# A gated bidirectional scan with a binarised linear layer: adding x to finished batches in six transfers of 512 tokens where there were twelve of 256

## The chip, the core and the metric

The kernel runs on one core of one Trainium2 chip. The time is the device time of one launch in microseconds (us), lower is better; a median of a few runs is given with the lowest and the highest. One more execution was taken with the hardware profiler, and every duration below is from that one. PE is the matrix engine, DVE the vector engine, ACT the scalar (activation) engine, POOL the GpSimd engine, SP the engine that only issues DMAs here. DMAs that SP issues go by one queue, which the profile calls q1 (hardware_dynamic), those that POOL issues by another, q0 (software_dynamic); both are worked off by the same 16 DMA engines.

## What is computed

All arrays are float32; x and the side input are 4 x 1024 x 1024 (batch, token, channel).

```python
def wkv(r, k, v, w, u, time_emb):            # r = x, k = v = side input
    tf = sigmoid(sum(time_emb))              # one number per batch
    decay = exp(-exp(w)) * (0.5 + 0.5 * tf)  # per batch and channel
    ek = exp(min(k, 30)); ekv = ek * v
    nf, df = scan over tokens: a = a * decay + ekv, b = b * decay + ek
    nb, db = the same, from the last token to the first
    euk = exp(min(u + k, 30))
    num = nf + nb - ekv + euk * v
    den = df + db - ek + euk
    return sigmoid(r) * num / max(den, 1e-8) * (0.8 + 0.2 * tf)

bw = where(weight >= 0, 1, -1) * mean(abs(weight), over inputs)
out = x + wkv(x, side, side, w, u, cond) @ bw.T + bias
```

## The kernel before, in words

**Blocks.** The main loop `for g in range(steps)` has 32 steps; block g is one batch (g // 8) and 128 channels (g % 8), with the channels on the partitions and the 1024 tokens along the row. Each block loads a column block of the side input (`load_k`, L102) and of x (`load_gate`, L107) on SP, turns them on PE (L266, L272), takes exponentials on ACT (L278, L284) and runs four scans of 1024 tokens on DVE: numerator forward and backward (L366, L379), denominator forward and backward. Each backward scan starts from one column that ACT computes (`act_edge`, L372, "edge_num" and "edge_den").

**The block before, in the same step.** In step g DVE also finishes the denominator of block g - 1 (L389) and applies its gate (L423). POOL adds the own term of block g - 1 to its numerator by an accumulating DMA (`dma_own_numerator`, L384, 512 KB), floors the denominator (`floor_den`, L396), clamps block g (`pool_clamp`, L346), splits block g - 2 for the matrix product (L438) and multiplies block g - 1 (`den_product` L416, `num_product` L419, `gated_product` L428). ACT takes the reciprocal by a logarithm and an exponential (`act_log` L404, `act_reciprocal` L411) and makes the upper part of block g - 2 (`act_hi`, L433).

**The linear layer.** When the eight blocks of a batch are done, PE forms 16 groups for it, each 512 tokens by 128 outputs (`pe_product`, L449), some two and a half in a step. ACT scales a group and adds the bias (`act_scale`, L461), PE turns it back (`pe_turn`, L469), and ACT copies it into one half of a staged tile (`act_leave`, L557, 512 tokens by 256 outputs). When the second half is in, SP stores the tile to `out` (`store`, L135, 512 KB). The pool `resid` of staged tiles has two buffers, so the first copy into a tile waits until the store before last has landed. The first three batches go this way; what is stored lacks x. The last batch is done after the loop in another form (`pe_wide_product`, L517), and its x is added on DVE.

**Adding x.** For the first three batches POOL issues DMAs that read rows of x and accumulate them into the same rows of `out`, in HBM (`add_x`, L140). The dictionary `adds` says in which step each is issued, two steps or more after the batch's groups: four for each batch, 256 tokens and 1 MB each, in steps 16, 18, 20 and 22 for the first batch and 24, 26, 28 and 30 for the second. The four of the third batch would fall in steps 32 and later and are issued after the loop. In a step, `add_x` stands right behind `dma_own_numerator(g - 1)` in POOL's order.

**Order.** Nothing is reordered: the program runs under `tc.manual_schedule()`, and each engine and each DMA queue takes its instructions in the order of the text. One place depends on `adds`: in a step that issues an add, `act_log` stands behind `act_edge` for the numerator on ACT, in a step without one ahead of it:

```python
if g > 0 and not adds[g]:
    act_log(g - 1)
...
act_edge(g, nums[g], "edge_num")
if g > 0 and adds[g]:
    act_log(g - 1)
```

Of the kernel before, what the change touches and what calls it, by code (L numbers as in the profile page):

```python
# [21 lines left out]
def kernel(  # L22
# [28 lines left out]
    P = 128  # L51
    B, T, C = x.shape
    TD = time_emb.shape[1]
    NT = T // P
    NC = C // P
    H = 512
    NH = T // H
# [4 lines left out]
    rows = ctx.enter_context(tc.tile_pool(name="rows", bufs=2))  # L62
# [73 lines left out]

    def add_x(b, n):

        rows = slice(2 * n * P, 2 * (n + 1) * P)
        nc.gpsimd.dma_start(  # L140
            out=out[b, rows, :], in_=x[b, rows, :], accum_op=ALU.add, max_dma_last_dim=8192
        )
# [418 lines left out]
    steps = B * NC  # L561
# [38 lines left out]

    adds = {g: [] for g in range(steps + 1)}
    for b in range(B - 1):
        for n in range(NT // 2):
            adds[min((b + 2) * NC + 2 * n, steps)].append((b, n))

# [9 lines left out]
    with tc.manual_schedule():  # L617
# [57 lines left out]
        for g in range(steps):  # L675
            b, cc = divmod(g, NC)
# [16 lines left out]
            for i in adds[g]:  # L693
                add_x(*i)
# [100 lines left out]
        for i in adds[steps]:  # L795
            add_x(*i)
# [43 lines left out]
        n = NT - 1  # L840
# [41 lines left out]
```

## Time and profile before

| | |
|---|---|
| time before | 489.85 us, median of 3 runs (489.81 to 491.19) |
| profiled execution: its own time, its span | 489.83 us, 488.0 us |
| busy, share of the span | DVE 97%, POOL 82%, PE 75%, ACT 69% |
| chain that ended last | DVE 75%, PE 17%, issue 3%, ACT 2% |
| x into `out` by accumulating DMA | 12 issues on POOL, 1024 KB each, 11.8 us from issue to landing (median) |
| own terms by accumulating DMA | 32 issues on POOL, 512 KB each, 5.6 us |
| staged tiles to `out` | 24 issues on SP, 512 KB each, 5.1 us |
| bytes moved | q1 59.78 MB, q0 29.37 MB |

The span is the time from the first to the last instruction of the profiled execution; the 1.8 us between it and the execution's time lie outside. A busy share is an average over all stages. The chain that ended last is followed back from the last instruction to whatever released each one, so an engine's share in it says how much of the time it held up the end. In rows of the profile, `out<-in` names what is written and read, and a wait is put down to the last of the things waited for.

### The profile page before, as it was taken

To read this page: it belongs to the slowest core of one execution; us is meant where nothing else is said; L and a number is where in the kernel's file an instruction comes from. 1 tells how busy PE (TensorE), PEld (TensorE's weight loads), DVE (VectorE), ACT (ScalarE), POOL (GpSimd) and SP (SyncE) were. 2 spreads that over 40 slices of the span, in tenths; PEclk is the share of its full clock that TensorE was granted. 3 is DMA by queue.
4 is the path that set the end of the run, shared out by engine and by line. 5 is a ranking of instruction groups with operands and counts; after the bars stand their busy time and mean duration, and the time that the engine had idled before them with its cause. 6 is when DMAs were issued, how large, how long until landed. Compare 5 with 4: busy or idle time off the path is not lost.

```text
span 488.0 us, 5214 instructions
## 1 busy us (share of the span) xinstructions
PE 363.9 (75%) x1813; PEld 296.9 (61%) x1813; DVE 474.9 (97%) x331; ACT 335.9 (69%) x466; POOL 402.2 (82%) x276
## 2 busy tenths in 40 slices
PE   3434433344588877778999998965999998989996
PEld 2333332233466666656777777744888777868885
DVE  6999999999999999999999999999999999999976
ACT  4795968869595967769697879697866979724000
POOL 3379999999999999999999999999999999991000
PEclk9975566666699999999999999985999999999999
DMA  8865565555455555559787996889569697899954
GB/s 227 246 173 146 156 174 141 137 141 140 112 147 150 147 141 139 147 139 254 177 208 161 264 235 173 167 213 221 126 108 277 151 271 213 188 229 284 235 198 176
DMA packets 89762, 89.49 MB, mean 183 GB/s; under 512 B 2660, under 2 KB 80776, under 8 KB 88200
## 3 DMA queue, kind: packets, MB, share of 16 engines
q1 hardware_dynamic: 83320, 59.78, 41.0%
q0 software_dynamic: 6400, 29.37, 31.6%
q8 instruction: 14, 0.23, 0.2%
q14 instruction: 12, 0.10, 0.1%
q10 hardware_dynamic: 16, 0.00, 0.0%
HBM read 55.59 MB, written 29.36 MB: 174 GB/s over the span
## 4 chain that ended last, share of the span: by engine, by line
DVE 75%; PE 17%; issue 3%; ACT 2%; POOL 0%; DMA 0%; SPq 0%; DVEq 0%; POOLq 0%; ACTq 0%
DVE num L379 13%; DVE den L379 13%; DVE den L366 13%; DVE num L366 12%; PE wide L517 8%; DVE den L389 7%; DVE num L350 6%; DVE den L423 6%; PE po L449 5%; DVE euk L356 4%; PE last L517 2%; PE bank L517 1%; PE sgT L272 1%; PE turned L469 1%; PE kT L266 1%
## 5 line engine op out<-in xcount | busy, mean ns | idle before, releaser
L449 PE MATMUL po<-gated,wT 128*128 128x512 f32 x768 | 199.7, 408 | 0.3 <-ACT staged L557 0.3
L449 PEld LDWEIGHTS po<-gated,wT 128*128 128x128 f32 x768 | 141.9, 192 | 30.4 <-ACT staged L557 0.8
L266 PE MATMUL kT<-ident,k_rows 128*128 128x128 f32 x248 | 42.1, 325 | 61.6 <-issue 43.0
L272 PE MATMUL sgT<-ident,sg_rows 128*128 128x128 f32 x256 | 43.2, 324 | 46.4 <-DVE den L423 41.2
L438 POOL TENSOR_TENSOR gated<-num,gated 128x512 fp32r<-128x512 f32 x60 | 75.6, 1280 | 2.4
L266 PEld LDWEIGHTS kT<-ident,k_rows 128*128 128x128 f32 x248 | 33.8, 167 | 69.4 <-issue 51.6
L379 DVE TENSOR_TENSOR_SCAN den<-bank,edge_den,den 128x1024 f32<-128x1024 f32 x32 | 74.8, 2339 | 0.4 <-ACT edge_den L372 0.4
L416 POOL TENSOR_TENSOR den<-den,eu 128x1024 f32<-128x1024 f32 x31 | 73.8, 2380 | 1.4 <-ACT eu L411 1.4
L379 DVE TENSOR_TENSOR_SCAN num<-bank,edge_num,num 128x1024 f32<-128x1024 f32 x32 | 74.8, 2337 | 0.0
L419 POOL TENSOR_TENSOR num<-num,eu 128x1024 f32<-128x1024 f32 x31 | 73.7, 2377 | 0.8 <-DMA num<-euk 0.8
L428 POOL TENSOR_TENSOR num<-den,num 128x1024 f32<-128x1024 f32 x30 | 71.8, 2393 | 2.8 <-DVE den L423 0.5
L366 DVE TENSOR_TENSOR_SCAN den<-bank,den 128x1024 f32<-128x1024 f32 x32 | 72.2, 2258 | 0.0
L366 DVE TENSOR_TENSOR_SCAN num<-bank,num 128x1024 f32<-128x1024 f32 x31 | 70.6, 2277 | 0.0
L272 PEld LDWEIGHTS sgT<-ident,sg_rows 128*128 128x128 f32 x256 | 35.1, 167 | 57.1 <-DVE den L423 29.7
L433 ACT CAST gated<-num 128x512 fp32r<-128x512 f32 x64 | 36.5, 618 | 30.2 <-POOL num L428 25.8
L396 POOL TENSOR_SCALAR den<-den,floor 128x1024 f32<-128x1024 f32 x31 | 36.8, 1188 | 20.7 <-DVE den L389 17.5
L404 ACT ACTIVATE eu<-den,gain 128x1024 f32<-128x1024 f32 (+1 forms) x33 | 36.9, 1121 | 20.8 <-POOL den L396 20.4
L517 PE MATMUL wide<-wT,gated 128*128 128x512 f32 x192 | 45.4, 393 | 2.1 <-POOL gated L438 2.1
L557 ACT COPY staged<-turned 128x512 f32<-128x512 f32 x48 | 27.5, 574 | 21.3 <-PE turned L469 21.3
L517 PEld LDWEIGHTS wide<-wT,gated 128*128 128x128 f32 x192 | 35.8, 188 | 10.2 <-POOL gated L438 2.5
L389 DVE SCALAR_TENSOR_TENSOR den<-eu,top,den 128x1024 f32<-128x1024 f32 (+1 forms) x33 | 41.5, 1260 | 0.0
L356 DVE SCALAR_TENSOR_TENSOR euk<-eu,top,kT 128x1024 f32<-128x1024 f32 x31 | 38.7, 1250 | 0.0
(91 smaller groups left out, 578.9 us busy)
## 6 DMA issues: line engine op xcount, KB each, us to landing
sg_rows<-in_x_dram SPq DMA_DIRECT2D x32, 512.0 KB, 5.9
num<-euk POOLq DMA_DIRECT2D x32, 512.0 KB, 5.6
k_rows<-in_fside_BxSxS_dram SPq DMA_DIRECT2D x31, 512.0 KB, 5.2
out_dram<-staged SPq DMA_DIRECT2D x24, 512.0 KB, 5.1
out_dram<-in_x_dram POOLq DMA_DIRECT2D x12, 1024.0 KB, 11.8
w_rows<-in_L_ffn_weight_dram SPq DMA_DIRECT2D x8, 512.0 KB, 5.7
x_rows<-in_x_dram SPq DMA_DIRECT2D x8, 512.0 KB, 11.5
out_dram<-x_rows SPq DMA_DIRECT2D x7, 512.0 KB, 2.6
```

Source lines behind the costliest of these rows:

```text
L266: nc.tensor.transpose(kT[:, s * P : (s + 1) * P], k_rows[g][:, s, :], ident)
L272: nc.tensor.transpose(t[:, s * P : (s + 1) * P], sg_rows[g][:, s, :], ident)
L356: nc.vector.scalar_tensor_tensor(euk, eus[g], top[:, b, cc : cc + 1], k_ps[g], ALU.min, ALU.mult)
L366: nc.vector.tensor_tensor_scan(t, decay_row(g), t, 0.0, ALU.mult, ALU.add)
L379: nc.vector.tensor_tensor_scan(back, decay_row(g), back, inits[g, which], ALU.mult, ALU.add)
L389: nc.vector.scalar_tensor_tensor(dens[g][:, ts], eus[g][:, ts], top[:, b, cc : cc + 1], dens[g][:, ts], ALU.min, ALU.add,)
L416: engine.tensor_mul(dens[g][:, ts], dens[g][:, ts], eus[g][:, ts])
L419: engine.tensor_mul(nums[g][:, ts], nums[g][:, ts], eus[g][:, ts])
L428: engine.tensor_mul(nums[g][:, ts], dens[g][:, ts], nums[g][:, ts])
L438: engine.tensor_sub(t[:, 1, :], nums[g][:, h * H : (h + 1) * H], t[:, 0, :].bitcast(F32))
L449: nc.tensor.matmul(prods[q], wT[:, cc, oc * P : (oc + 1) * P], gated[b, cc, h][:, i, :], start=(cc == 0 and i == 0), stop=(cc == NC - 1 an ...
L517: nc.tensor.matmul(t, gated[last, cc, h][:, i, s * P : (s + 1) * P], wT[:, cc, cols], start=(cc == 0 and i == 0), stop=(cc == NC - 1 and i ...
```

## The change

Twelve adds of 256 tokens become six of 512 tokens (2 MB each). They are issued in steps 16 and 20 for the first batch, 24 and 28 for the second, and two after the loop for the third. The same rows get the same x. In steps 18, 22, 26 and 30 no add is issued any more, and by the condition quoted above `act_log` stands ahead of `act_edge` there. The order of every other instruction on every engine is as before. POOL's instruction for an add names 256 rows of 2048 elements where it named 128.

```diff
     def add_x(b, n):
 
-        rows = slice(2 * n * P, 2 * (n + 1) * P)
+        rows = slice(n * H, (n + 1) * H)
         nc.gpsimd.dma_start(
             out=out[b, rows, :], in_=x[b, rows, :], accum_op=ALU.add, max_dma_last_dim=8192
         )
...
     adds = {g: [] for g in range(steps + 1)}
     for b in range(B - 1):
-        for n in range(NT // 2):
-            adds[min((b + 2) * NC + 2 * n, steps)].append((b, n))
+        for n in range(NH):
+            adds[min((b + 2) * NC + 4 * n, steps)].append((b, n))
```

Here P = 128, H = 512, NT = 8, NH = 2, NC = 8, B = 4, steps = 32.

## The prediction, made before the changed kernel ran

> **What bounds the kernel now.** I read the page first: busy shares, the chain that ended last, the DMA issues.
>
> ```profile
> span 488.0 us, 5214 instructions
> PE 363.9 (75%) x1813; PEld 296.9 (61%) x1813; DVE 474.9 (97%) x331; ACT 335.9 (69%) x466; POOL 402.2 (82%) x276
> ...
> DVE 75%; PE 17%; issue 3%; ACT 2%; POOL 0%; DMA 0%; SPq 0%; DVEq 0%; POOLq 0%; ACTq 0%
> ...
> out_dram<-staged SPq DMA_DIRECT2D x24, 512.0 KB, 5.1
> out_dram<-in_x_dram POOLq DMA_DIRECT2D x12, 1024.0 KB, 11.8
> ```
>
> DVE works without a break; no DMA is on the chain. So an add costs nothing by its bytes, only by what it makes late for DVE. How much slack there is stands in the timeline; first DVE and POOL in steps 15 (no add) and 16 (add), two views:
>
> ```profile
> 208.76 1.27 DVE L389 SCALAR_TENSOR_TENSOR den<-eu,top,den 128x1024 f32<-128x1024 f32 x1
> 217.77 1.19 DVE L423 SCALAR_TENSOR_TENSOR den<-den,sgT 128x1024 f32<-128x1024 f32 x1
> 222.25 1.28 DVE L389 SCALAR_TENSOR_TENSOR den<-eu,top,den 128x1024 f32<-128x1024 f32 x1
> 231.26 1.19 DVE L423 SCALAR_TENSOR_TENSOR den<-den,sgT 128x1024 f32<-128x1024 f32 x1
> 235.75 1.32 DVE L389 SCALAR_TENSOR_TENSOR den<-eu,top,den 128x1024 f32<-128x1024 f32 x1
> ```
>
> ```profile
> 215.01 2.40 POOL L416 TENSOR_TENSOR den<-den,eu 128x1024 f32<-128x1024 f32 x1
> 222.16 0.89 POOL L384 DMA_DIRECT2D num<-euk  x1
> 222.76 1.19 POOL L140 DMA_DIRECT2D out_dram<-in_x_dram  x1
> 228.80 2.40 POOL L416 TENSOR_TENSOR den<-den,eu 128x1024 f32<-128x1024 f32 x1
> ```
>
> A step lasts from one L389 to the next, 13.50 us. L423 needs L416. Without an add L416 ends at 217.41, 0.36 us before L423; with one at 231.20, 0.06 before it. POOL is nearly a second bound in steps with an add.
>
> Then the DMA queues around the add of step 28 (issued at 385.33, landed 397.3), in the stretch 390 to 395, and ACT and DVE behind it:
>
> ```profile
> q0 software_dynamic: 102, 0.84, 96.9%
> q1 hardware_dynamic: 102, 0.10, 7.7%
> ```
>
> ```profile
> 398.51 0.59 ACT L557 COPY staged<-turned 128x512 f32<-128x512 f32 x1 [3.18 <-PE turned L469]
> 399.00 0.78 ACT L461 ACTIVATE z<-po,wub,out_scale 128x512 f32<-128x512 f32 x1
> ...
> 402.06 0.28 ACT L372 ACTIVATE edge_num<-num,edge 128x1 f32<-128x1 f32 x1
> ```
>
> ```profile
> 402.97 2.34 DVE L379 TENSOR_TENSOR_SCAN num<-bank,edge_num,num 128x1024 f32<-128x1024 f32 x1
> ```
>
> While the add runs, the engines take one packet of q1 (1 KB, of a staged tile's store) for each packet of the add (8 KB): 102 against 102. So the store issued at 386.40 landed 11.75 us later, at 398.15, where the median store takes 5.1. The copy L557 at 398.51 refills that store's buffer (two buffers, so it waits for the store before last). The profile puts its wait on PE, which was ready last, but the store landed only 0.36 us earlier.
>
> **POOL's part.** The issue of a 2 MB add names 256 rows for 128. Issued behind L384, which ends at 223.05, the old one ends at 223.95: 0.90 us for 128 rows. The cheapest issue on POOL, L622 with 8 rows, took 0.58. Twice the rows therefore cost between 0 more (all fixed) and 0.90 (all by rows); I take 0.31, the difference of the two rows, as that is what 120 rows cost. L416 has 0.06, 0.06, 0.23 and 0.04 to spare in steps 16, 20, 24 and 28, so L423 waits 0.25 + 0.25 + 0.08 + 0.27 = 0.85 us in all; by the bounds 0 and 3.2.
>
> Four steps lose their add. Steps 18, 19, 22, 23, 26, 27 and 30 exceed 13.50 by 0.05, 0.09, 0.03, 0.08, 0.05, 0.10 and 0.01 (a late L423 in the add's step, then an L389 of 1.32 to 1.38 us instead of 1.27), and L389 of step 31 by 0.11: 0.5 us comes back. Net of POOL +0.3, bounds -0.5 and +2.7.
>
> ACT's new order in these four (logarithm ahead of the edge) is that of every step without an add: in step 17 the logarithm ended at 239.57, the edge column at 239.75, and the scan that needs it began at 240.37. Nothing, with 0.6 us of cover; beyond that DVE would wait.
>
> **The transfer's part.** Each add gets 128 packets of 8 KB more. Alone, q0 moved 1.28 MB in the stretch 226 to 232, so 1.05 MB takes 4.9 us; beside a store, 102 packets in 5 us, so 6.3 us. What queues behind it:
>
> On q0, the own-term DMA of the next step. After step 16: the add landed at 233.93, would at 238.8, and 0.52 MB more at the same rate end near 241.3; the DMA landed at 241.7 anyway, and POOL's L419 wants it at 244.42. After step 28: 397.3 + 6.3 + 2.5 = 406.1, wanted at 407.00. No wait, with 0.9 us of cover at the tightest.
>
> On q1, loads and stores. Loads are asked for a step and more ahead; the closest, the k load issued at 386.89 (landed 399.98), would land near 407 where PE wants it at 403.1, but the wait on ACT below is as long and covers it. Stores: after step 16 the store of 232.17 has until the copy at 251.01; after step 20 that of 286.35 (landed 289.95) until 299.34, and 289.95 + 6.3 + 2.5 = 298.8 just makes it; around step 24 there are no stores between 327 and 360. After step 28 the store of 386.40 has 0.36 us and gets at least 4.9 more: it lands at 403.05 to 404.4 if it follows the add, and 2.5 us later, up to 406.9, if the own-term DMA, which POOL issues at 398.53 into the same queue as the add, also goes ahead. I take 405.0, the middle. ACT stands in L557 until then, with L461, L433, L404 and L372 queued behind it; L372 ended at 402.34 for a scan at 402.97, so DVE's wait is the landing less 398.51 less 0.63: 3.9 to 7.8 us, at 405.0 it is 5.9. POOL and PE are late by as much and no more.
>
> [...]
>
> The two adds after the loop carry the bytes of the four; those landed by 467.1, 21 us before the end, so nothing.
>
> Sum, on the profiled execution's 489.83 us (span 488.0 and 1.8 outside; the median is 489.85): + 5.9 + 0.3 = 496.0. With the ends of both terms, 3.4 and 10.5, it is 493.2 to 500.3.
>
> **Rivals.** *The store is not held (ends level).* Place: the store of step 28. If q1's packets get more turns beside the longer add than one in two, it lands in time. It decides at 399.1 (398.51 + 0.63): landing before that, DVE waits for nothing and only POOL's +0.3 is left, 490.1 us, at its bounds 489.3 and 492.5. For it: in the stretch 402 to 405 q1 got 583 packets beside 117 of q0, though those were 512-byte loads against 4 KB packets. Against: 102 to 102 with this very kind of store.
>
> *POOL as the bound.* If generating descriptors goes by rows, 0.90 an issue, the four steps cost 2.7 net, beside the 5.9: 498.4 us. For it: four adds issued in a row after the loop ended 0.83 to 0.90 apart, as work by rows would. Against: 0.58 for 8 rows.
>
> *More than one store late.* The store of 286.35 has 0.5 us to spare. If it comes 2 us late, some 1.4 us more, 497.4.
>
> A gain of 1.5 us is not in sight: all steps together exceed 13.50 by 0.8 us.
>
> **How the numbers follow.** A measurement here can tell 0.3%, 1.5 us. One held store: 0.62, time 496.0. Held store and a dear issue or a second late store: 0.13, 497 to 500. Store not held: 0.22, 489.3 to 492.5, mostly within 1.5 us of before. Something that I don't see, to the good: 0.03. So slower 0.77 (with a tenth of the third case, its upper end), same 0.20, faster 0.03. The range 489.7 to 499.0 leaves out the lower third of the third case and the top of the second, some 0.15; the likeliest case's own is 493.2 to 499.
>
> **What would show it.** In the changed profile: ACT's idle time before one L557 in step 29 of 7 us or more, put down to the store's DMA, with a landing of 17 us or more for the store issued at the start of step 28; right behind it DVE idle at L379 for edge_num by 4 to 8 us, the only long idle of DVE in the loop; L423 waiting 0.1 to 0.3 us in steps 16, 20, 24 and 28; adds that land some 17 us after issue; steps 18, 22, 26 and 30 at 13.50. I am wrong if that store lands within 13 us, or if DVE's idle time lies elsewhere, at L423 above all.

## The result, and the profile after

| | before | after |
|---|---|---|
| median | 489.98 us, 4 runs (489.81 to 491.19) | 497.59 us, 4 runs (495.72 to 497.85) |
| profiled execution: its own time, its span | 489.83 us, 488.0 us | 497.68 us, 495.9 us |
| end of the loop (begin of the L389 behind step 31) | 438.00 us | 444.30 us |
| from there to the span's end | 50.0 us | 51.6 us |

The changed kernel is 1.4% slower: ratio 1.0142, interval 1.0112 to 1.0171. Of the profiled 7.9 us, 6.3 are in the loop and 1.6 behind it. The page first: its span, busy shares, chain, the group of the backward numerator scan, and DMA issues.

```profile
span 495.9 us, 5207 instructions
PE 369.0 (74%) x1813; PEld 300.0 (60%) x1813; DVE 475.1 (96%) x331; ACT 335.5 (68%) x466; POOL 396.9 (80%) x270
...
DVE 63%; PE 18%; ACT 7%; DMA 5%; issue 4%; POOL 1%; SPq 0%; POOLq 0%; DVEq 0%; ACTq 0%
...
L379 DVE TENSOR_TENSOR_SCAN num<-bank,edge_num,num 128x1024 f32<-128x1024 f32 x32 | 74.9, 2341 | 6.0 <-ACT edge_num L372 6.0
...
out_dram<-staged SPq DMA_DIRECT2D x24, 512.0 KB, 3.6
out_dram<-in_x_dram POOLq DMA_DIRECT2D x6, 2048.0 KB, 18.8
```

DVE is busy as long as before (475.1 us against 474.9) and POOL 5 us less. No engine got more to do (PE's 5 us more are the same 1813 products); DVE waits more, 6.0 us of it at L379 for the column that ACT computes. DMA stands on the chain with 5%, where it had nothing. The median store even became faster (3.6 us); the one issued at the start of step 28 took 17.3. DVE's waits, as engine, line, what ended the wait, us in total, times, longest:

```profile
DVE num L379 <- ACT edge_num L372: 6.0, 3, 4.3
DVE wide L539 <- PE wide L517: 3.7, 1, 3.7
...
DVE den L416 <- ACT eu L411: 1.6, 1, 1.6
```

Before, L379 for edge_num was not in this list, and the last two stood at 3.2 and 0.5. L423, where a late POOL would show, does not appear. The three waits at L379 in DVE's timeline:

```profile
254.65 2.35 DVE L379 TENSOR_TENSOR_SCAN num<-bank,edge_num,num 128x1024 f32<-128x1024 f32 x1 [0.62 <-ACT edge_num L372]
...
408.15 2.35 DVE L379 TENSOR_TENSOR_SCAN num<-bank,edge_num,num 128x1024 f32<-128x1024 f32 x1 [4.29 <-ACT edge_num L372]
...
422.87 2.35 DVE L379 TENSOR_TENSOR_SCAN num<-bank,edge_num,num 128x1024 f32<-128x1024 f32 x1 [1.06 <-ACT edge_num L372]
```

They are in steps 18, 29 and 30. In the lengths of the steps (the table below), 4.43 us of the loop's 6.3 are in step 29, 1.13 in step 30, 0.64 and 0.27 in steps 18 and 26, and the other steps together are 0.2 us shorter. What stood ahead of the second on ACT:

```profile
404.60 0.58 ACT L557 COPY staged<-turned 128x512 f32<-128x512 f32 x1 [8.46 <-DMA out_dram<-staged]
405.08 0.78 ACT L461 ACTIVATE z<-po,wub,out_scale 128x512 f32<-128x512 f32 x1
405.75 1.14 ACT L433 CAST gated<-num 128x512 fp32r<-128x512 f32 x2
406.78 1.16 ACT L404 ACTIVATE eu<-den,gain 128x1024 f32<-128x1024 f32 x1
407.83 0.29 ACT L372 ACTIVATE edge_num<-num,edge 128x1 f32<-128x1 f32 x1
```

This is the chain that was forecast: the copy of step 29 waits 8.46 us for the buffer whose store was issued in step 28, and four things queue behind it on ACT, the edge column last. The store's own answer (line L135, the stretch 386 to 388), and the share of the queues while it lay there (391 to 401: packets, MB, share of the engines):

```profile
who waited for it (us, times):
  ACT staged L557: 8.5, 1
...
DMA to landing us min/median/max: 17.3/17.3/17.3
```

```profile
q0 software_dynamic: 229, 1.88, 95.7%
q1 hardware_dynamic: 205, 0.21, 7.7%
```

Packets take turns one for one again: in 10 us q1 moved 0.21 MB of its store in packets of 1 KB while the add moved 1.88 MB in packets of 8 KB. Near-equal sums would also come of turns of several packets each; the trace's list of packets settles it: each of the 205 packets of q1 is followed by one of q0 that starts 0.04 to 0.08 us later. The add, issued at 386.09, landed at 403.75, the store right behind it at 404.52.

The store was not the only transfer held. The profile's chain, followed back from the end, meets not the store but the k load that SP issued right behind it (start, us):

```profile
387.70 21.05 DMA k_rows<-in_fside_BxSxS_dram
```

From there it goes by PE (L266, the products of L449, the turn L469) to the copy L557 of step 29's end on ACT, and by the gates and the logarithm of step 30 to the edge column for which DVE waits 1.06 us there. DVE's 4.29 us in step 29 ended with the store, its 1.06 in step 30 came by way of the k load.

### The profile page after: what moved, and what is told of

The parts are those of the page before. It is cut to its first block, busy times and chain, and to the rows that moved or that the text cites. A ratio compares the mean times of both kernels' runs of the same rounds, so it can differ in the third digit from the quotient of the medians.

```text
span 495.9 us, 5207 instructions
## 1 busy us (share of the span) xinstructions
PE 369.0 (74%) x1813; PEld 300.0 (60%) x1813; DVE 475.1 (96%) x331; ACT 335.5 (68%) x466; POOL 396.9 (80%) x270
## 4 chain that ended last, share of the span: by engine, by line
DVE 63%; PE 18%; ACT 7%; DMA 5%; issue 4%; POOL 1%; SPq 0%; POOLq 0%; DVEq 0%; ACTq 0%
DVE den L366 11%; DVE den L379 11%; DVE num L379 11%; DVE num L366 10%; PE wide L517 8%; DVE den L389 6%; DVE num L350 5%; DVE den L423 5%; PE po L449 5%; DMA k_rows<-in_fside_BxSxS_dram 4%; DVE euk L356 3%; PE last L517 2%; ACT sg_rows L111 1%; ACT eu L404 1%; PE kT L266 1%
## 5 line engine op out<-in xcount | busy, mean ns | idle before, releaser
L449 PE MATMUL po<-gated,wT 128*128 128x512 f32 x768 | 201.7, 411 | 0.9 <-POOL gated L438 0.6
L449 PEld LDWEIGHTS po<-gated,wT 128*128 128x128 f32 x768 | 142.9, 194 | 31.7 <-POOL gated L438 1.1
L266 PE MATMUL kT<-ident,k_rows 128*128 128x128 f32 x248 | 42.9, 330 | 62.5 <-issue 42.2
L379 DVE TENSOR_TENSOR_SCAN num<-bank,edge_num,num 128x1024 f32<-128x1024 f32 x32 | 74.9, 2341 | 6.0 <-ACT edge_num L372 6.0
L266 PEld LDWEIGHTS kT<-ident,k_rows 128*128 128x128 f32 x248 | 34.6, 170 | 70.5 <-issue 53.9
L416 POOL TENSOR_TENSOR den<-den,eu 128x1024 f32<-128x1024 f32 x31 | 73.7, 2378 | 2.2 <-ACT eu L411 2.1
L379 DVE TENSOR_TENSOR_SCAN den<-bank,edge_den,den 128x1024 f32<-128x1024 f32 x32 | 74.9, 2341 | 0.4 <-ACT edge_den L372 0.4
L428 POOL TENSOR_TENSOR num<-den,num 128x1024 f32<-128x1024 f32 x30 | 71.8, 2394 | 2.8 <-DVE den L423 0.5
L396 POOL TENSOR_SCALAR den<-den,floor 128x1024 f32<-128x1024 f32 x31 | 35.8, 1155 | 26.0 <-DVE den L389 20.5
L517 PE MATMUL wide<-wT,gated 128*128 128x512 f32 x192 | 46.7, 401 | 2.0 <-POOL gated L438 2.0
L557 ACT COPY staged<-turned 128x512 f32<-128x512 f32 x48 | 27.5, 573 | 27.6 <-PE turned L469 19.1
L517 PEld LDWEIGHTS wide<-wT,gated 128*128 128x128 f32 x192 | 36.8, 193 | 10.5 <-POOL gated L438 2.4
L389 DVE SCALAR_TENSOR_TENSOR den<-eu,top,den 128x1024 f32<-128x1024 f32 (+1 forms) x33 | 41.4, 1256 | 0.0
```

The costliest lines, as they stand in the source:

```text
L266: nc.tensor.transpose(kT[:, s * P : (s + 1) * P], k_rows[g][:, s, :], ident)
L379: nc.vector.tensor_tensor_scan(back, decay_row(g), back, inits[g, which], ALU.mult, ALU.add)
L389: nc.vector.scalar_tensor_tensor(dens[g][:, ts], eus[g][:, ts], top[:, b, cc : cc + 1], dens[g][:, ts], ALU.min, ALU.add,)
L416: engine.tensor_mul(dens[g][:, ts], dens[g][:, ts], eus[g][:, ts])
L428: engine.tensor_mul(nums[g][:, ts], dens[g][:, ts], nums[g][:, ts])
L449: nc.tensor.matmul(prods[q], wT[:, cc, oc * P : (oc + 1) * P], gated[b, cc, h][:, i, :], start=(cc == 0 and i == 0), stop=(cc == NC - 1 an ...
```

## Experiments

Lengths of the steps that differ (from one L389 to the next, us) and the median with all times' bounds. "Waits at L416" is DVE's wait after the loop. The kernel before was timed again beside them: medians of 489.87 (23 runs), 489.98 (23) and 489.97 (17, beside e12), all from 489.5 to 491.5.

| kernel | 18 | 26 | 29 | 30 | L416 waits | time |
|---|---|---|---|---|---|---|
| before | 13.56 | 13.55 | 13.59 | 13.51 | 0.5 | 489.98 |
| after | 14.20 | 13.82 | 18.02 | 14.64 | 1.6 | 497.59 (495.72 to 497.85) |
| e1_split_last | 14.20 | 13.92 | 13.58 | 13.62 | 1.5 | 492.08 (490.83 to 492.23) |
| e5_merge_last_alone | 13.52 | 13.56 | 17.47 | 13.85 | 0.5 | 494.03 (493.92 to 494.59) |
| e2_old_order | 13.50 | 13.49 | 17.45 | 13.75 | 0.5 | 494.09 (493.82 to 495.53) |
| e3_new_order_alone | 14.20 | 13.84 | 13.58 | 13.49 | 1.6 | 491.10 (490.36 to 492.11) |
| e9_later_old_order | 13.51 | 13.77 | 13.53 | 13.60 | 0.5 | 489.96 (489.44 to 491.56) |
| e7_packets_2k | 14.20 | 13.82 | 17.19 | 15.02 | 1.5 | 497.83 (496.78 to 498.79) |
| e10_filled_after | 14.21 | 13.83 | 17.62 | 15.15 | 0.5 | 495.74 (495.64 to 496.31) |
| e11_filled_before | 13.56 | 13.53 | 13.58 | 13.50 | 0.5 | 489.75 (489.63 to 490.12) |
| e12_late_and_filled | 13.50 | 13.50 | 13.53 | 13.60 | 0.5 | 489.84 (489.68 to 490.41) |

### The held store: one add split back, one add merged alone

*e1_split_last* is the changed kernel with the last add inside the loop as two of 256 tokens again.

```diff
-        rows = slice(n * H, (n + 1) * H)
+        rows = slice(n[0] * 2 * P, n[1] * 2 * P)
...
-            adds[min((b + 2) * NC + 4 * n, steps)].append((b, n))
+    for g, b, n in (
+        (16, 0, (0, 2)), (20, 0, (2, 4)), (24, 1, (0, 2)),
+        (28, 1, (2, 3)), (30, 1, (3, 4)), (32, 2, (0, 2)), (32, 2, (2, 4)),
+    ):
+        adds[g].append((b, n))
```

> The changed kernel, with only the last add inside the loop split again into two of 256 tokens in steps 28 and 30 (step 30 so gets its old ACT order back, as it issues an add). Held store (A): the 4.4 us that DVE lost at L379 in step 29 go, with the 1.1 us of step 30 and the 1.6 us by which the part after the loop grew; left are 0.64 in step 18 and 0.27 in step 26: 497.6 - 7.1 = 490.5 us, 489.8 to 491.3, and no idle time of ACT before L557 that a store ends. Price of the merged transfers wherever they stand (B: descriptors on POOL, or the own-term DMA behind the add): three of four merged adds stay, so three quarters of the 7.6 us, 495.7 us.

Measured: 492.08 us, ratio to before 1.0026 (1.0014 to 1.0038). The store landed after 11.6 us, no copy waited for it, and steps 29 and 30 were back at 13.58 and 13.62. Steps 18 and 26 stayed long. The time is above the 489.8 to 491.3 expected, since 8 of the 12 runs (492.0 to 492.2) have the longer part behind the loop that is treated below; the other four are at 490.8 to 490.9.

*e5_merge_last_alone* is the converse: the kernel before, only its adds of steps 28 and 30 merged in step 28, and the old order on ACT.

```diff
-            adds[min((b + 2) * NC + 2 * n, steps)].append((b, n))
+    # rows and loop as in e1; n counts 256 tokens: one each in steps 16 to 26, then
+        (28, 1, (2, 4)), (32, 2, (0, 1)), (32, 2, (1, 2)), (32, 2, (2, 3)), (32, 2, (3, 4)),
...
-    if g > 0 and adds[g]:
+    if g > 0 and (g >= 2 * NC and g % 2 == 0):
         act_log(g - 1)
```

> The kernel before, with only the adds of steps 28 and 30 made one of 512 tokens in step 28; ACT's old order kept everywhere. A: step 29 alone loses 4.4 us, and the part after the loop may lose its 1.6 again: 490.0 + 4.4 to 6.0 = 494.4 to 496.0 us, with the store issued at the start of step 28 landing 17 us later. B: one merged add of four, 490.0 + 1.9 = 491.9 us.

Measured: 494.03 us, ratio 1.0074 (1.0059 to 1.0090). The store took 16.8 us. Of ACT's waits and DVE's in this kernel:

```profile
ACT staged L557 <- DMA out_dram<-staged: 8.0, 1, 8.0
...
DVE num L379 <- ACT edge_num L372: 3.8, 1, 3.8
```

One merged add out of four brings the wait at L379 and some 4.1 us (494.03 less 489.9); the place is shown from both sides.

### The order on ACT

*e2_old_order* is the changed kernel with the logarithm behind the edge column in all even steps from 16 on, as before; *e3_new_order_alone* is the kernel before, its twelve adds kept, with the logarithm ahead in steps 18, 22, 26 and 30.

```diff
 # e2, in the changed kernel
-    if g > 0 and not adds[g]:
+    if g > 0 and not (g >= 2 * NC and g % 2 == 0):
         act_log(g - 1)
 # e3, in the kernel before
-    if g > 0 and not adds[g]:
+    if g > 0 and not (g >= 2 * NC and g % 4 == 0):
         act_log(g - 1)
```

> The changed kernel, with ACT's logarithm behind the edge column in every even step from 16 on, as before the change. If the new order costs what steps 18, 26 and 30 show (C): DVE's waits at L379 in steps 18 (0.7), 26 (0.3) and 30 (1.1) go, step 29 keeps its 4.3: 497.6 - 2.1 = 495.5 us; if the 1.1 of step 30 only follow from step 29's delay, 496.7. If the order costs nothing, as predicted: 497.6.

> The kernel before, with all twelve adds where they were, and only ACT's order in steps 18, 22, 26 and 30 changed to logarithm ahead of edge column. Here POOL's floor is 0.3 us later in those steps than without an add, so the logarithm cannot start earlier than in the changed kernel. C: DVE waits at L379 in steps 18 and 26 at least, 0.5 to 1.5 us each: 490.0 + 1 to 4 = 491 to 494 us. If the order costs nothing: 490.0.

Measured: e2 494.09 us, ratio 1.0072 (1.0056 to 1.0089), which is e5's time and 1.4 below the expected 495.5, as the longer part behind the loop did not come; the order costs 1.65 us (against 495.74 of e10 below, which is free of that part too). e3 491.10, ratio 1.0018 (1.0005 to 1.0030): steps 18 and 26 grow by 0.64 and 0.29, step 30 does not. (Its runs fall into two groups, 490.4 to 491.2 and 491.8 to 492.1; the lower is about one us above the lower group of the kernel before.) So about one us is the order by itself, and the rest arises in step 30, which ACT enters late behind the held transfers of step 29: with the old order the step takes 13.75, with the new one 14.64. ACT's timeline shows why step 18 pays; first the changed kernel, then the kernel before with the scan on DVE:

```profile
247.77 2.01 ACT L111 ACTIVATE sg_rows<-sg_rows 128x1024 f32<-128x1024 f32 x2
249.80 1.28 ACT L94 ACT_TABLE_LOAD   x1
251.09 0.58 ACT L557 COPY staged<-turned 128x512 f32<-128x512 f32 x1
251.58 0.78 ACT L461 ACTIVATE z<-po,wub,out_scale 128x512 f32<-128x512 f32 x1
252.25 1.14 ACT L433 CAST gated<-num 128x512 fp32r<-128x512 f32 x2
253.28 1.15 ACT L404 ACTIVATE eu<-den,gain 128x1024 f32<-128x1024 f32 x1
254.34 0.28 ACT L372 ACTIVATE edge_num<-num,edge 128x1 f32<-128x1 f32 x1
```

```profile
253.19 0.30 ACT L372 ACTIVATE edge_num<-num,edge 128x1 f32<-128x1 f32 x1
253.39 1.14 ACT L404 ACTIVATE eu<-den,gain 128x1024 f32<-128x1024 f32 x1
```

```profile
253.87 2.34 DVE L379 TENSOR_TENSOR_SCAN num<-bank,edge_num,num 128x1024 f32<-128x1024 f32 x1
```

ACT works without a break here. Step 17, as most odd steps, ends with the gates of two blocks and two table loads (L111, L94), so ACT comes 1.7 us late into step 18 (251.08 against the step's L389 at 249.39). The edge column is ready at 254.62 and the scan begins at 254.65; without the logarithm ahead it would have been ready about 1.06 earlier (254.34 less 253.28). Step 22 has no copy L557 in that queue; its edge column ended at 308.31, 0.50 before its scan, and the step took 13.50. Step 26 pays for another reason: no gates stand in step 25, but its copy L557 waits 3.8 us for PE in either kernel, and in the kernel before the column ended 0.54 before its scan.

e2's profile holds one more event, in step 22: an own-term DMA landed late, POOL multiplied late, and DVE's L389 ran beside it.

```profile
300.66 2.40 POOL L419 TENSOR_TENSOR num<-num,eu 128x1024 f32<-128x1024 f32 x1 [1.84 <-DMA num<-euk]
303.14 2.38 POOL L428 TENSOR_TENSOR num<-den,num 128x1024 f32<-128x1024 f32 x1
```

```profile
303.67 2.94 DVE L389 SCALAR_TENSOR_TENSOR den<-eu,top,den 128x1024 f32<-128x1024 f32 x1
```

L389 took 2.94 us for the usual 1.28 and the step 15.16. That execution is the one of 495.53 us, the other five are at 493.8 to 494.3; the changed kernel's own profile has no such step, and no time of e12's 12 runs, with the same large adds up to step 24, is more than 0.8 us above the lowest. So it belongs to a single execution; why that DMA was late is open.

### Do merged adds cost anything else?

*e9_later_old_order*: all six adds stay merged, the one of step 28 is issued in step 29, and ACT has the old order.

```diff
-            adds[min((b + 2) * NC + 4 * n, steps)].append((b, n))
     # rows and loop as in e1
+        (16, 0, (0, 2)), (20, 0, (2, 4)), (24, 1, (0, 2)),
+        (29, 1, (2, 4)), (32, 2, (0, 2)), (32, 2, (2, 4)),
...
-    if g > 0 and adds[g]:
+    if g > 0 and (g >= 2 * NC and g % 2 == 0):
         act_log(g - 1)
```

> The changed kernel, with the add of step 28 issued one step later, in step 29, where SP has fewer loads to ask for, and ACT's old order in the even steps. A: the store at the start of step 28 goes unhindered and lands within 6 us; the next store that meets the add, in step 29, has until the copy in step 30, 14 us after it. With the order's cost gone as well, what is left is the kernel before: 489.5 to 490.2, or 491.3 where the part after the loop takes its longer form. If merged adds cost by themselves (B): four of them, 495 us or more.

Measured: 489.96 us, ratio 0.9999 (0.9984 to 1.0013). The store of step 28 landed after 5.5 us, and no copy waited for a store. The whole loss in the loop is thus one place and one order; the 2 MB at a stretch, POOL's larger issues and the two large adds after the loop cost nothing that shows within that interval, some 0.7 us. (Step 26 of the profile, 13.77 with the old order, is an L423 that waited 0.16 us for POOL and a longer L389; e12, with the same adds and order, has 13.50.)

### Smaller packets

*e7_packets_2k* asks whether the packet's size decides: the adds are cut into packets of 512 elements, 2 KB, so that one turn of q0 is about a quarter as long (by the shares of the queues 0.18 us a packet in the row of 396 to 400 below, 0.67 in that of the changed kernel above).

```diff
-            out=out[b, rows, :], in_=x[b, rows, :], accum_op=ALU.add, max_dma_last_dim=8192
+            out=out[b, rows, :], in_=x[b, rows, :], accum_op=ALU.add, max_dma_last_dim=2048
```

> The changed kernel, with its 512-token adds cut into packets of 2 KB instead of 8 KB (1024 rows of 512 elements in POOL's instruction). Held store, one packet for one (A): the store issued at the start of step 28 needs 512 turns of the add's 1024 instead of outlasting its 256, so it lands some 9 to 11 us after issue, not 17, before the copy that refills its buffer; ACT's 8.5 us idle and DVE's 4.3 us at L379 in step 29 go. POOL's issue may cost more: 0.05 us per 128 rows (1.18 to 1.23 from before to after) makes 0.3 us an add, 1.2 in all. Together 497.6 - 4.4 + 1.2, with or without the 1.1 of step 30: 493.3 to 494.4. If q1 is held back by the add's bytes or time and not by packets: the landing stays at 17 us and the time at 497.6 or above.

Measured: 497.83 us, ratio 1.0149 (1.0127 to 1.0171): as slow as the changed kernel, against the expectation. The store itself was free, 6.0 us to landing (issued 388.42), but the loss stayed. DVE's waits, and the row on ACT behind the largest:

```profile
DVE den L379 <- ACT edge_den L372: 4.0, 2, 3.5
...
DVE num L379 <- ACT edge_num L372: 2.3, 3, 1.4
...
DVE den L423 <- POOL den L416: 1.3, 4, 0.4
```

```profile
411.67 1.02 ACT L278 ACTIVATE den<-kT 128x1024 f32<-128x1024 f32 x1 [5.37 <-PE kT L266]
```

The next in line took the store's place. The k load issued right behind it landed 20.6 us later, PE turned it late, ACT stood at L278 and with it the other edge column. In the changed kernel that load was as late:

```profile
408.89 1.94 PE L266 MATMUL kT<-ident,k_rows 128*128 128x128 f32 x8 [2.32 <-DMA k_rows<-in_fside_BxSxS_dram]
```

It landed 21.1 us after its issue, its cost in step 29 hidden under the store's. Taking one waiter away was worth next to nothing: steps 29 and 30 together took 32.2 us here and 32.7 in the changed kernel. And the turns were by packet with the smaller packets too: in 396 to 400 of e7,

```profile
q0 software_dynamic: 329, 0.67, 90.5%
q1 hardware_dynamic: 328, 0.17, 21.0%
```

Again each of the 328 packets of q1 is followed by one of q0, here within 0.05 us. The store escaped because it passed before the add came: in 391 to 393 q1 moved 410 packets and q0 10. So this run does not show what smaller packets would do to a store that does queue beside them. Issuing the add with four times the rows took POOL 1.64 us for 1.24, which is the wait at L423 above and 0.3 to 0.4 us in each of steps 16, 20, 24 and 28.

### The microseconds behind the loop

The changed kernel's profile lost 1.6 us after the loop. Rows of the stretches by window (from:to, length, busy us of PE, PEld, DVE, ACT, POOL, granted PE clock, DMA share, GB/s), and PE's timeline:

```profile
434.40:437.40 3.00, 1.04 (x5) 0.56 (x4) 3.00 (x3) 2.37 (x3) 2.86 (x3) 1.00 0.99 232
437.40:441.00 3.60, 3.60 (x11) 2.83 (x10) 3.60 (x3) 0.07 (x1) 3.60 (x3) 0.54 0.95 308
441.00:446.00 5.00, 5.00 (x26) 4.11 (x26) 4.96 (x5) 0.22 (x1) 4.47 (x4) 0.99 0.93 191
```

```profile
436.91 1.01 PE L517 MATMUL wide<-wT,gated 128*128 128x512 f32 x3 [1.96 <-POOL gated L438]
```

PE stood still for 1.96 us, and in the 3.6 us that followed it had half its clock: 11 products, where 17 ran in as long a stretch of e10 below. In the kernel before, PE stands still for 2.10 us at the same place and in the profiled execution kept its full clock:

```profile
430.62 0.96 PE L517 MATMUL wide<-wT,gated 128*128 128x512 f32 x3 [2.10 <-POOL gated L438]
```

```profile
431.00:434.60 3.60, 3.60 (x17) 2.96 (x16) 3.60 (x3) 0.00 (x0) 3.60 (x3) 1.00 1.05 272
```

Its times, however, fall into two groups, 12 of one set of 23 runs at 489.5 to 490.0 and 11 at 491.1 to 491.4, some 1.5 us apart (28 of all 63 runs are in the upper one); those of the changed kernel are three at 497.5 to 497.9 and one at 495.7. To see whether these are one thing, ten products of wide (2, 0) are done once more in the final step ahead of their place, which fills the standstill and leaves the result as it is: *e10_filled_after* in the changed kernel, *e11_filled_before* in the kernel before.

```diff
+                open_wide(2, 0)
+                for cc in range(NC - 3):
+                    for i in range(2):
+                        nc.tensor.matmul(
+                            wide[2, 0], gated[last, cc, 0][:, i, 2 * P : 3 * P], wT[:, cc, :H],
+                            start=(cc == 0 and i == 0), stop=(cc == NC - 4 and i == 1),
+                        )
                 pe_wide_product(2, 0, range(NC - 3))
```

> The changed kernel, with the first ten products of one output tile made twice in the last step, the first time for nothing, so that PE does not stand still for 2 us ahead of the last blocks. The profiles of the changed kernel and of the first and third experiment have a stretch of 3.4 us at half the granted clock right after that standstill, and DVE waits 1.5 to 1.6 us for the last reciprocal there; those without the stretch wait 0.5. If the standstill brings the half clock (D): the longer form goes, 495.7 us in every run. If not: 497.6 in most runs, or more by the 2.4 us of added products if these lie on the path.

> The kernel before with the same ten products made twice. Its runs have fallen at 489.7 (14 of 23) and 491.3 (9 of 23). D: all runs at 489.7, none at 491.3. If the standstill is not the cause: the same two groups, or all later by up to 2.4 us.

Measured: e10 495.74 us (ratio 1.0111, 1.0094 to 1.0127), all five runs at 495.6 to 496.3; e11 489.75 (ratio 0.9987, 0.9977 to 0.9997), all twelve at 489.6 to 490.1. The upper group is gone from both. The same stretch in e10, by window:

```profile
436.40:440.00 3.60, 3.60 (x17) 2.91 (x16) 3.60 (x3) 0.41 (x1) 3.60 (x3) 1.00 1.02 290
```

So PE's standstill brings half a clock in some executions, at 1.5 to 1.9 us each, in either kernel. It is no price of the change by itself; whether the change makes it likelier (3 of 4 runs against 28 of 63) is too few runs to say. Its share does differ between kernels: by their times 8 of 12 runs of e1 have it, none of the 12 of e2 and e5. So medians that hold it are not to be set against medians that don't. Compared without it, the change costs 495.74 - 489.75 = 6.0 us.

### Everything together

*e12_late_and_filled* is e9 with the ten products.

> The changed kernel's six merged adds, the last in-loop one in step 29 and not 28, the old order on ScalarE in even steps, and the ten products of wide (2, 0) done once more ahead of their place in the final step. Theory (the held store and the order are the only prices of the change in the loop, the half clock after PE's standstill the only price behind it): 489.7 us in nearly all runs, between 489.4 and 490.2, 0.1% below the median of the kernel before, as the kernel before with the same ten products gave (489.75). Rival (merged adds cost something that the late place only masked): 490.5 to 491.5, or a second group of runs near 491.3.

Measured: 489.84 us, 12 runs from 489.68 to 490.41, ratio 0.999 (0.9979 to 1.0). Merged adds, one step later and with the old order, are level with the kernel before (0.1 us above e11, which has the same filling). The one version whose interval lies below 1 is e11, by 0.13%, and that is the filled standstill, not the adds.

## Why the prediction was right, and where not

The prediction said 496.0 us, by one held store; 497.59 was measured, 495.74 without the half clock. The mechanism and its place are shown by e1, e5 and e9. That the sum came out within 0.3 us of 495.74 is luck: one term was 1.6 us too large, and one that was put at nothing cost 1.65.

- **The held store**: 5.9 us forecast, 4.3 measured (4.43 more in step 29; e2's 494.09 less 489.8). The term that was too large is the landing: 405.0 was the middle between a store that follows the add and one that also lets the own-term DMA go ahead, 18.6 us after its issue at 386.40. It took 17.3 (387.21 to 404.52), 1.3 less: the own-term DMA did not go ahead of it (it landed at 407.62). The time 404.52 is close to 405.0 only since steps 18 and 26 had put store and scan 0.8 to 0.9 us later alike. The other 0.3 is ACT, which went from L557 to the column's end in 3.52 us where the row of before gave 3.83.
- **ACT's order in steps 18, 22, 26 and 30**: "Nothing, with 0.6 us of cover" is the step that failed. It cost 1.65 us. I read the cover in step 17 and took it for all. Step 17 is odd; step 18 follows the two gates and the table loads, and ACT enters it without slack. The row that counted stood in the trace of before: L372 at 253.19 in step 18, ACT without a gap ahead of it, for a scan at 253.87: 0.38 us between the column's end and the scan, and a logarithm of 1.06 to be put in front, which makes 0.68 for the 0.64 that the step lost.
- **POOL**: 0.31 us forecast for each doubled issue, 0.05 measured (median 1.24 for 1.18 us). L423 never waited, so the sign for it (0.1 to 0.3 us in four steps) did not come, and the net of +0.3 was near -0.2. With e7's 1.64 for 1024 rows, a row costs about 0.5 ns and nearly all of an issue is fixed; the row I took as nearest, 8 rows at 0.58, is a plain load and not an accumulating DMA. The rival of POOL by rows is out.
- **The k load**: "the wait on ACT below is as long and covers it" was right for step 29, but it was the second of two holds of nearly one size, as e7 showed, and with the new order what was left of it cost DVE about 1 us in step 30. I had weighed it for a wait of its own and not as what remains when the first is gone.
- **After the loop**: no term, as it should be for the change; the 1.6 us of the profile are the half clock, which one profile of before does not show and its times do (491.19 was among the three I had).
- **The turns**: one packet for one was read from sums, 102 to 102, and the lists of packets of the changed kernel and of e7 agree: one to one, whether the add's packets had 8 KB (205 of q1, 229 of q0) or 2 KB (328 and 329 in e7). The sums alone would fit turns of several each as well. The rates taken for the add (1.28 MB alone in 226 to 232 of the kernel before, 214 GB/s, and 102 packets of 8 KB in 5 us beside a store) placed its landing: 17.7 us after issue, for 16.9 to 18.3 by the forecast.

The rivals: the store was held; a second late store did not come (only one DMA wait on L557). The signs were right for L557 (8.46 us for at least 7), the landing (17.3 for at least 17), DVE's wait at L379 (4.3 for 4 to 8) and the adds (17.0 to 19.2 us in the loop), wrong for L423 and for steps 18, 26 and 30 at 13.50.

## What to carry to other kernels

Making a background transfer larger cost nothing here by its bytes (489.96 us in e9 beside 489.98) and 4 us by where it stood (494.03 in e5): a small transfer that queued beside it got one packet for each of the large one's (205 beside 229 in 10 us). So look for what is issued just behind it and is waited for within its length, list every such waiter and not only the first, and move the issue (e9) rather than cut it into smaller packets (497.83 us in e7). Where a condition moves an instruction on an engine, read the slack in each of the steps that it moves in, not in one like them. When times of a kernel fall into two groups (489.5 to 490.0 and 491.1 to 491.4 here), look in the profile for a standstill of PE (2.10 us here) before a change is charged with the gap.

## What the runs showed of the hardware

- **Half a clock after a standstill of 2 us, in some executions.** In its last steps the changed kernel's PE had half its clock twice: 3.6 us (0.54) after the standstill of 1.96, and in 407 to 414 (0.51) after standstills of 2.87 and 2.32 in step 29. (Both kernels have it around 330 too, 0.50 in 330 to 334, about a standstill of 6.0 us, where DVE does not wait for PE.) After a standstill of 2.10 the profiled execution of the kernel before kept its full clock (1.00). Filling the standstill (1.96, and 2.10 in the kernel before) took the upper group of times away in all 17 runs of e10 and e11, where 28 of 63 runs of the kernel before were in it. The slow stretch lasted 3.4 us at 0.50 in e1 and e3 and some 7 in step 29; why it comes in some executions and not in others is open.
- **One packet for one**, with packets of 8 KB against 1 KB (229 and 205) as with 2 KB against 512 bytes (329 and 328): the queue with the smaller packets moved bytes about in the ratio of the sizes, 0.21 MB beside 1.88 and 0.17 beside 0.67. Beside the own-term DMA it was not so: in 403 to 405 of the changed kernel q1 moved 540 packets and q0 65, and why is open.
- **An issue on POOL is nearly all fixed**: 1.18 us for 128 rows, 1.24 for 256, 1.64 for 1024.
- **DVE's L389 beside POOL's L428**: 2.94 us for 1.28, in the one step (22 of e2) where they ran side by side for 1.9 us; where only the last 0.3 us of L428 reached into L389 (398.31 in the kernel before), it took 1.36.
